# Adding the experts' weighted results into one row per token by indirect DMA

## The chip, the core and the metric

The kernel runs on one core of a Trainium2 chip. A core has a matrix engine (TensorE, PE in the profile; PEld is its weight load), VectorE (DVE), ScalarE (ACT), GpSimd (POOL) and SyncE (SP), which each run their own queue of instructions in order, and sixteen DMA engines that all queues share. DMAs issued by SyncE go out on a hardware queue (q1), those issued by GpSimd on a software queue (q0) whose descriptors GpSimd itself makes. The metric is the device time of one execution in microseconds (us), lower is better.

## The reference

The network has two layers on an image of 2 x 256 x 64 x 64: area attention and an LSTM, then convolutions with a state-space mixer, and at last a mixture of experts over the 8192 tokens. Only the last part is touched by the change:

```python
B, T, D, H, E = (16, 4096, 256, 512, 8)
xf = x.reshape(-1, Dd)
logits = xf @ gate_w + gate_b
probs = jax.nn.softmax(logits, axis=-1)
top2_vals, top2_idx = jax.lax.top_k(probs, 2)
cw = jnp.zeros((N, Ee)).at[jnp.arange(N)[:, None], top2_idx].add(top2_vals)
def step(acc, params):
    w1, bb1, w2, bb2, we = params
    h = jax.nn.gelu(xf @ w1 + bb1, approximate=False)
    y = h @ w2 + bb2
    return (acc + we[:, None] * y, None)
out, _ = jax.lax.scan(step, zeros_like(xf), (W1, b1, W2, b2, cw.T))
...
t = _to_tokens(x)
t = t + _L1_ffn_ref(_ln_t(t), ...)
x = _from_tokens(t, x)
```

The tokens are normalised, each goes to its two best of eight experts (256 to 512 to 256, GELU between), the two results are weighted by the softmax of the gate, summed and added to the token, and the tokens are turned back into channels by rows.

## The kernel before

`body` runs the attention, then the LSTM with the mixers, then `experts` (a second, conditional run of the last two exists for a guess that fails; it is skipped here). `experts` has three stages: `route`, `run_blocks`, `combine`. There T = 8192 tokens, P = 128 partitions, TILES = 64 tiles of 128 tokens, K = 4 tiles to a group, C = 256 channels.

**route.** `normalise` (L1949) turns the tokens group by group on TensorE, takes gate logits and statistics, and then `scale` (L2007) writes the normalised tokens: three tiles of a group on ScalarE, one on GpSimd, and one DMA of 0.52 MB by SyncE to the DRAM tensor `rows` (L2019). All sixteen `scale` groups stand after the second square root (L2084). `choose` picks the two best experts on VectorE. Then a table is built (L2221 to L2239) that says which token stands at which place: the assignments are sorted by expert into blocks of RB = 256 places, and one-hot products on TensorE, made by VectorE and ScalarE in sixteen rounds, fill `table`. Three blocks' weights are fetched before the table (L2210). `exponents` (L2109) comes behind it: ScalarE loads the exponential's table, makes the exponentials and loads GELU's. VectorE at last turns the table into the indices `xi` (rows to gather) and `ri` (rows to put).

**run_blocks(0, 68).** One block is 256 places of one expert; 2 x 8192 places need at most 71 blocks, of which 68 always run. The order is written out by hand. For block i TensorE does `turn` (transposes of the gathered rows `xg`), `up` (eight 128-row products into `ph`, GELU on ScalarE) and `down` (products into `py`); `up` of block i is interleaved with `down` of block i - 1. VectorE copies `xt` and adds the bias in `y`. GpSimd's queue has, for each block, the first put of 128 rows (L2323), the weights three blocks ahead (L2320, issued at L2125), the second put, and the two gathers of a later block (L2275). `results` has a row of its own for every (token, choice), and spare rows for empty places, so no two puts touch the same row: all are declared in one group "results" without dependences among them (L2328), and no put waits for another. Buffers: 3 for `xg`, 3 for `y`, 3 + 1 for the weights. During blocks 8 and 12 to 43 VectorE also computes the weights (`weigh`, L2116, sent through DRAM by two DMAs) and lays the tokens out by channels (`lay_out`, L2365).

**combine.** For each of sixteen groups of 512 tokens SyncE reads two tiles of `results` (both wait for all puts, L2380), ScalarE scales the first by its weight, VectorE multiplies and adds the second (L2387), TensorE transposes (L2391), VectorE adds the laid-out residual (L2397), and GpSimd issues the output's DMA (L2401).

Of the kernel before, what the change touches and what calls it, by code (L numbers as in the profile page):

```python
# [1861 lines left out]
def experts(tc, sh, ap, out, half, left):  # L1862
# [19 lines left out]
    with ExitStack() as ctx:  # L1882
        cp = ctx.enter_context(tc.tile_pool(name="e_const", bufs=1))
        dp = ctx.enter_context(tc.tile_pool(name="e_dram", bufs=1, space=bass.MemoryType.DRAM))
        rows = dp.tile([T, C], F32, name="rows")
        results = dp.tile([2 * T + NBLK * RB, C], F32, name="results")
        by_rows = dp.tile([T, 2], F32, name="by_rows")

        x = cp.tile([P, 2, WW, P], F32, name="x_turned")

        placed = sh.x.rearrange("p c b n -> p (c b n)").rearrange("p (c m w) -> p c m w", c=2, w=WW)

# [31 lines left out]
        weights = cp.tile([P, TILES, 2], F32, name="weights")  # L1924
        by_row = cp.tile([P, TILES // K, K, 2], F32, name="by_row")

        spare = iota("spare", [P, J, NBLK], [[P, J], [RB, NBLK]], base=2 * T + TILES, step=1)

# [20 lines left out]
        def normalise(p2, logits, halves):  # L1949


            with ExitStack() as own:
# [54 lines left out]
                def scale(g):  # L2007
                    xt = p2.tile([P, K, C], F32, name="xt")
                    for k in range(K):
                        t = g * K + k  # L2010
                        if k == K - 1:
                            nc.gpsimd.tensor_scalar(
                                xt[:, k], tok[:, t], inv[:, t : t + 1], less[:, t : t + 1], ALU.mult, ALU.add
                            )
                        else:
                            nc.scalar.activation(
                                xt[:, k], tok[:, t], AF.Identity, scale=inv[:, t : t + 1], bias=less[:, t : t + 1]
                            )
                    nc.sync.dma_start(rows.rearrange("(p w) d -> p w d", w=TILES)[:, group(g)], xt)  # L2019

# [29 lines left out]
                for g in range(TILES // K):  # L2050
# [24 lines left out]
                    if g == 13:  # L2075
                        ready = take_gates(*gates(2))
                        root_in(1)
                last = gates(3)
                root(1)
# [3 lines left out]
                turn_gates(*ready)  # L2083
                for g in range(TILES // K):  # L2084
                    scale(g)
# [23 lines left out]
        def exponents(pr):  # L2109

            nc.scalar.activation(one, going[:, 0, 0:1], AF.Exp)
            nc.scalar.activation(ex, pr, AF.Exp)
            nc.scalar.activation(best, best, AF.Exp)
            nc.scalar.activation(total[:, 0:1], sh.eps5, AF.Gelu)

        def weigh():  # L2116
            nc.vector.tensor_reduce(total, ex, AX.X, ALU.add)
            nc.vector.reciprocal(total, total)
            nc.vector.tensor_scalar(weights[:, :, 0], total, one, None, ALU.mult)
            nc.vector.tensor_tensor(weights[:, :, 1], best, total, ALU.mult)  # L2120
            nc.sync.dma_start(by_rows.rearrange("(p w) i -> p w i", w=TILES), weights)
            nc.sync.dma_start(by_row, by_rows.rearrange("(g p k) i -> p g k i", p=P, k=K))

# [11 lines left out]
        def route():  # L2135
            with ExitStack() as own:
# [12 lines left out]


                both = p1.tile(full, BF16, name="both")
                nc.vector.tensor_tensor(both, picks[0], picks[1], ALU.add)
# [56 lines left out]
                for i in range(3):  # L2209
                    fetch_weights(i)  # L2210


# [8 lines left out]
                for t0 in range(0, TILES, K):  # L2221
# [5 lines left out]
                    named = wide[t0 // K % 2][:, : 2 * size].rearrange("p (k i c n) -> p k i c n", k=K, i=2, c=2)  # L2227
                    nc.scalar.mul(named[:, :, :, 1], high.rearrange("p k n i -> p k i n"), me1)
                    for t in range(t0, t0 + K):
                        for i in range(2):  # L2230
# [9 lines left out]
                for _ in range(WARM_UP):  # L2240
                    nc.tensor.matmul(rest[:, :RB], every, place, start=True, stop=True)
                exponents(pr)
                tile_of, inner = (table[:, :, k * NB : k * NB + NBLK] for k in range(2))
                tokens = p1.tile([P, J, NBLK], F32, name="tokens")

                nc.vector.tensor_scalar(tokens, tile_of, float(TILES), float(T - TILES), ALU.is_ge, ALU.mult)
                nc.vector.tensor_tensor(tokens, tokens, tile_of, ALU.add)
                nc.vector.scalar_tensor_tensor(tokens, inner, float(TILES), tokens, ALU.mult, ALU.add)
# [3 lines left out]
                nc.vector.tensor_scalar(xi, ri, T - 1, None, ALU.bitwise_and)  # L2252

        puts = []
        landed = mybir.DependencyInfo(mybir.DependencyClass.Sync, mybir.DependencyReason.DATA)

        def run_blocks(lo, hi):
            with ExitStack() as own:
# [13 lines left out]
                def fetch(i):  # L2272
                    xg = fetched[i] = p3.tile([P, J, C], F32, name="xg")
                    for j in range(J):
                        gather(xg[:, j], rows, xi[:, j, i : i + 1])  # L2275

                def turn(i):
                    xg, wt = fetched.pop(i), weights_of.pop(i)
                    px = ps.tile([P, 2, RB], F32, name="px")
                    for c in range(2):  # L2280
# [4 lines left out]
                    if lo == 0 and i < 2:  # L2285
                        keep_busy(FILL + 2)
                    return xt, wt

                def up(xt, wt, alone):

# [11 lines left out]

                def down(i, act, wt, then):
                    py = ps.tile([P, J, C], F32, name="py")
# [11 lines left out]
                    nc.vector.tensor_tensor(y, py, b2, ALU.add)  # L2316
                    for j in range(J):

                        if j == 1 and then is not None:
                            fetch_weights(then, extra)  # L2320
                        elif j == 1 or then is None:
                            nc.gpsimd.memset(between, 0.0)
                        put = nc.gpsimd.indirect_dma_start(  # L2323
                            out=results, out_offset=bass.IndirectOffsetOnAxis(ap=ri[:, j, i : i + 1], axis=0),
                            in_=y[:, j], in_offset=None,
                        ).ins

                        tc.declare_no_dep(put, group="results", reason="different rows")  # L2328
                        tc.add_to_no_dep_group("results", put)
                        puts.append(put.name)  # L2330

# [6 lines left out]
                for i in range(lo, hi):  # L2338
# [16 lines left out]
                    for _ in below:  # L2355
                        pass
                    below = i, act, now[1]
                    if i == 8:
                        weigh()
                    if 12 <= i < 12 + 2 * T // TB:  # L2360
                        lay_out(*divmod(i - 12, 2))
                for _ in down(*below, None):
                    pass

        def lay_out(j, c):  # L2365

            rows_ = slice(j * TB // WW, (j + 1) * TB // WW)
            nc.vector.tensor_copy(placed[:, c, rows_], x[:, c, :, rows_].rearrange("p w m -> p m w"))

        def combine():  # L2370
            with ExitStack() as own:
# [3 lines left out]
                for g in range(T // TB):  # L2375
                    b, n0 = g * TB // N, g * TB % N
                    y = [p4.tile([P, K, C], F32, name=f"y{i}") for i in range(2)]
                    for i in range(2):
                        at = i * T + g * TB
                        got = nc.sync.dma_start(y[i], results[at : at + TB].rearrange("(p k) d -> p k d", k=K))  # L2380
                        for put in puts:
                            tc.add_manual_dep(got.ins, put, landed, reason="all results first")

                    po = ps.tile([P, 2, P, K], F32, name="po")
                    for k in range(K):
                        nc.scalar.activation(y[0][:, k], y[0][:, k], AF.Copy, scale=by_row[:, g, k, 0:1])
                        nc.vector.scalar_tensor_tensor(  # L2387
                            y[1][:, k], y[1][:, k], by_row[:, g, k, 1:2], y[0][:, k], ALU.mult, ALU.add
                        )
                        for c in range(2):  # L2390
                            nc.tensor.transpose(po[:, c, :, k], y[1][:, k, c * P : c * P + P], sh.ident)  # L2391
                    cut = slice(n0, n0 + TB)
                    res = p2.tile([P, 2, TB], F32, name="res")
                    before = placed[:, :, g * TB // WW : (g + 1) * TB // WW]
                    parts = [slice(0, 2)] if g < T // TB - 1 else [slice(0, 1), slice(1, 2)]
                    for eng, cs in zip((nc.gpsimd, nc.sync), parts):
                        nc.vector.tensor_tensor(  # L2397
                            res[:, cs], po[:, cs].rearrange("p c m k -> p c (m k)"),
                            before[:, cs].rearrange("p c m w -> p c (m w)"), ALU.add,
                        )  # L2400
                        eng.dma_start(out[b, :, cut].rearrange("(c p) n -> p c n", p=P)[:, cs], res[:, cs])  # L2401

# [149 lines left out]
```

## Time and profile before

| what | value |
|---|---|
| time, median of 3 runs | 2808.76 us (2808.6 to 2810.47) |
| the profiled execution's own time | 2817.78 us |
| its span, mean granted TensorE clock | 2815.9 us, 0.969 |
| DMA over the span | 399.14 MB, 142 GB/s |
| software queue q0 | 71488 packets, 293.00 MB, 44.1% of 16 engines |
| `experts`, from the first transposes to the end | about 2116 to 2816 us |
| first gather of `rows`, first put | 2206.62, 2232.84 us |
| `y<-results` issues | 32, of 512 KB, 2740.7 to 2786.0 us |

How to read it: an answer of the trace names an instruction by engine, line of the kernel, operation and tiles as `out<-in`; `xN` is how many. A time in brackets behind a row is how long the engine sat idle before it, and `<-` names what ended that wait. "Issue" is time in which an engine waited for nothing that the profile shows. The chain of waits follows the work that ended last back to its cause.

### The profile page before, as it was taken

Reading aid. Unit: us, or ns where it says so; the run is one execution under the profiler, and the core shown is the slowest. Engines: PE = TensorE matmul, PEld = TensorE weight load, DVE = VectorE, ACT = ScalarE, POOL = GpSimd, SP = SyncE. Lnnn points to the kernel's source line nnn. Section 1 sums busy time; section 2 is a strip of 40 time slices with the busy share of each in tenths; the row PEclk is TensorE's granted clock in tenths of the full one; section 3 lists DMA queues with packets and bytes.
Section 4 is the critical chain, followed back from the end, with each engine's and each line's share of the span. In section 5 each row is a group of like instructions: output and inputs, shape, how many; then the busy total and the mean of one; then the engine's idle time right before and its main releaser. Section 6 shows DMA issues by size and latency. Waiting matters only on the chain.

```text
span 2815.9 us, 45486 instructions
## 1 busy us (share of the span) xinstructions
PE 2582.6 (92%) x16873; PEld 1468.9 (52%) x16873; DVE 1921.1 (68%) x3693; ACT 1554.5 (55%) x2659; POOL 1276.2 (45%) x1214
## 2 busy tenths in 40 slices
PE   7899999999999999997899999868885899999984
PEld 2233333333333333331799999624444788888863
DVE  4788888888888888877666767698888322222116
ACT  2567677776777676664554555676637422222223
POOL 1354545444445545444312000287762366666651
PEclk9999999999999999999999999999997999999995
DMA  3566767676776767777450000045544266666658
GB/s 135 98 132 131 137 130 142 131 138 130 135 139 131 139 132 136 135 136 146 148 214 27 24 24 7 12 124 142 150 128 161 100 232 223 220 230 231 221 177 342
DMA packets 111226, 399.14 MB, mean 142 GB/s; under 512 B 20169, under 2 KB 24657, under 8 KB 101265
## 3 DMA queue, kind: packets, MB, share of 16 engines
q0 software_dynamic: 71488, 293.00, 44.1%
q1 hardware_dynamic: 38272, 98.87, 10.8%
q10 hardware_dynamic: 1232, 4.25, 0.4%
q8 instruction: 135, 2.21, 0.3%
q14 instruction: 99, 0.80, 0.1%
HBM read 178.81 MB, written 49.09 MB: 81 GB/s over the span
## 4 chain that ended last, share of the span: by engine, by line
PE 77%; DVE 10%; ACT 4%; issue 4%; DMA 3%; POOL 2%; SPq 0%; DVEq 0%; another core or an unknown queue 0%; POOLq 0%; ACTq 0%
PE ps L302 10%; PE ph L2296 9%; PE av_o L416 8%; PE po L170 8%; PE py L2308 8%; PE ps L403 7%; PE z L869 7%; PE z L829 6%; PE ps L398 3%; DVE hs L1744 2%; PE yp L1754 2%; DMA sx<-ex 2%; PE po L182 1%; DVE more L318 1%; PE po L416 1%
## 5 line engine op out<-in xcount | busy, mean ns | idle before, releaser
L372 DVE SCALAR_TENSOR_TENSOR acc<-vh,w_pe,acc 128x1008 f32<-128x1008 f32 (+7 forms) x384 | 482.2, 1259 | 8.3
L620 POOL DMA_DIRECT2D sx<-ex x320 | 279.6, 968 | 450.1 <-ACT ex L410 181.9
L410 ACT ACTIVATE ex<-ps 128x1024 f32<-128x1024 f32 x384 | 374.0, 1026 | 134.2 <-issue 54.3
L318 DVE CUSTOM_DVE_ANT_0 more<-ps,more 128x512 f32<-128x512 f32 x480 | 303.0, 687 | 132.1 <-PE ps L302 126.6
L2298 ACT ACTIVATE act<-ph,wt 128x256 f32<-128x256 f32 x272 | 129.2, 475 | 394.7 <-PE ph L2296 373.0
L2284 DVE COPY xt<-px 128x512 f32<-128x512 f32 x68 | 47.0, 692 | 395.7 <-PE px L2282 382.9
L2296 PE MATMUL ph<-xt,wt 128*128 128x256 f32 x1088 | 287.9, 387 | 5.5 <-ACT act L2298 4.0
L403 PE MATMUL ps<-q,k 32*128 32x512 f32 x2048 | 285.9, 600 | 0.0
L2308 PE MATMUL py<-wt,act 128*128 128x256 f32 x1088 | 278.7, 379 | 0.0
L615 POOL TENSOR_TENSOR sx<-sx,ex 128x1024 f32<-128x1024 f32 x64 | 153.1, 2391 | 221.2 <-PE ps L302 173.3
L314 ACT ACTIVATE more<-ps 128x1024 f32<-128x1024 f32 x240 | 233.5, 1029 | 16.7 <-ACT sx L410 5.9
L2296 PEld LDWEIGHTS ph<-xt,wt 128*128 128x128 f32 x1088 | 188.4, 189 | 66.1 <-DVE xt L2284 23.2
L416 PE MATMUL av_o<-ex,vt 128*32 128x512 f32 x1536 | 213.4, 608 | 6.2 <-ACT ex L410 6.2
L2308 PEld LDWEIGHTS py<-wt,act 128*128 128x128 f32 x1088 | 201.6, 190 | 24.7
L838 ACT ACTIVATE t<-z,bias 128x128 f32<-128x128 f32 x468 | 135.6, 365 | 124.2 <-PE z L869 122.8
L2323 POOL DMA_INDIRECT results<-y,ri x136 | 138.4, 1017 | 137.6 <-DVE y L2316 101.2
L302 PE MATMUL ps<-k,q 32*128 32x512 f32 x1088 | 183.4, 639 | 1.9 <-DVE nm L308 1.4
L869 PE MATMUL z<-xs,v 128*128 128x128 f32 x1512 | 180.9, 276 | 4.1 <-DVE xs L885 3.3
L829 PE MATMUL z<-xs,u 128*128 128x128 f32 x1536 | 183.5, 277 | 0.7 <-ACT xs L1003 0.7
L869 PEld LDWEIGHTS z<-xs,v 128*128 128x128 f32 x1512 | 174.1, 192 | 12.7 <-DVE xs L885 11.3
L829 PEld LDWEIGHTS z<-xs,u 128*128 128x128 f32 x1536 | 178.1, 193 | 0.9 <-ACT xs L1003 0.9
L1751 POOL TENSOR_TENSOR cs<-hs,cs 128x1024 f32<-128x1024 f32 x63 | 148.8, 2364 | 55.5 <-DVE hs L1744 37.1
(464 smaller groups left out, 4609.5 us busy)
## 6 DMA issues: line engine op xcount, KB each, us to landing
sx<-ex POOLq DMA_DIRECT2D x320, 512.0 KB
cs<-c_rows SPq DMA_DIRECT2D x128, 256.0 KB
y<-results SPq DMA_DIRECT2D x32, 512.0 KB
x<-xrows SPq DMA_DIRECT2D x8, 1024.0 KB
rows<-xt SPq DMA_DIRECT2D x16, 512.0 KB
out_x<-res POOLq DMA_DIRECT2D x15, 512.0 KB
xrows<-xn SPq DMA_DIRECT2D x24, 256.0 KB
u_rows<-xs SPq DMA_DIRECT2D x14, 384.0 KB
```

The source lines that it names most:

```text
L302: made.append(nc.tensor.matmul(tiles[h // 2][:, h % 2], qs[G, i // HM][head(h), i % HM * P : (i % HM + 1) * P], keys[head(h)], start=True, ...
L314: nc.scalar.activation(held["more"][j], tiles[j], AF.Relu)
L318: nc.vector.tensor_tensor_reduce(more, tiles[h // 2][:, h % 2], more, -1.0, 3.0e38, ALU.add, ALU.min, accum_out=nms[G][:, 0, h, i : i + 1],)
L372: mark(nc.vector.scalar_tensor_tensor(part, vh[:, c, 2 + r0 + dy : 2 + r1 + dy, w0 + dx : w1 + dx], w_pe[:, c, k : k + 1], part, ALU.mult, ...
L403: nc.tensor.matmul(tiles[h // 2][:, h % 2], k[head(h), m % HM * P : (m % HM + 1) * P], qs[G, n][head(h)], start=False, stop=True, tile_pos ...
L410: nc.scalar.activation(exs[i], tiles[i], AF.Exp, scale=HD**-0.5)
L416: nc.tensor.matmul(to[head(h)], lhs, exs[h // 2][:, h % 2], start=first, stop=last, tile_position=(0, HD * h))
L620: nc.gpsimd.dma_start(total[i], exs[i], accum_op=ALU.add)
L829: nc.tensor.matmul(z[c][:, g, :m], u[:, k, c, g], xin[j][:, k], start=g == GATES[0] and k == 0, stop=False, skip_group_check=True,)
L869: nc.tensor.matmul(z[c][:, g, :m], v[:, k, c, g], h[:, k], start=False, stop=k == 1, skip_group_check=True,)
L2296: nc.tensor.matmul(ph[:, hc], wt[:, at : at + P], xt[:, c], start=c == 0, stop=c == 1)
L2308: nc.tensor.matmul(py[:, j], act[:, hc, j * P : j * P + P], wt[:, at : at + C], start=hc == 0, stop=hc == NH - 1,)
```

## The change

Each token gets one row in `results`, which is filled with the token itself (the residual) before the blocks run (`keep_tokens`); the puts add into it by an accumulating indirect DMA. So `results` shrinks to 8192 rows and 256 spare ones. The weights of the two choices are computed on GpSimd in the table stage and stored in two more columns of `rows`, of which the second holds the difference of the weights; a gather brings them along, and VectorE scales `y` by the place's weight before the put. The puts of one block form a group, so that blocks are ordered among each other. Four `scale` groups and the exponentials move ahead. The combining stage reads one tile a group, transposes, and copies out on VectorE and ScalarE.

```diff
-        rows = dp.tile([T, C], F32, name="rows")
-        results = dp.tile([2 * T + NBLK * RB, C], F32, name="results")
-        by_rows = dp.tile([T, 2], F32, name="by_rows")
+        CW = C + 2
+        rows = dp.tile([T, CW], F32, name="rows")
+        results = dp.tile([T + RB, C], F32, name="results")
+        by_tile = rows.rearrange("(p w) d -> p w d", w=TILES)
...
-        spare = iota("spare", [P, J, NBLK], [[P, J], [RB, NBLK]], base=2 * T + TILES, step=1)
+        spare = iota("spare", [P, J, NBLK], [[P, J], [0, NBLK]], base=T + TILES, step=1)
+        second = cp.tile([P, J, NBLK], F32, name="second")
...
-                    nc.sync.dma_start(rows.rearrange("(p w) d -> p w d", w=TILES)[:, group(g)], xt)
+                    nc.sync.dma_start(by_tile[:, group(g), :C], xt)
...
                         root_in(1)
+                        scale(0)
+                for g in range(1, 4):
+                    scale(g)
                 last = gates(3)
...
-                for g in range(TILES // K):
+                for g in range(4, TILES // K):
                     scale(g)
...
-            nc.scalar.activation(total[:, 0:1], sh.eps5, AF.Gelu)
+            nc.scalar.activation(work[:, 0, 0:1], sh.eps5, AF.Gelu)
+            for n in (E // 2, E // 4, 1):
+                to = ex[:, :, :n] if n > 1 else total.unsqueeze(2)
+                nc.gpsimd.tensor_tensor(to, ex[:, :, :n], ex[:, :, n : 2 * n], ALU.add)
 
         def weigh():
-            nc.vector.tensor_reduce(total, ex, AX.X, ALU.add)
             nc.vector.reciprocal(total, total)
...
+            nc.gpsimd.tensor_scalar(weights[:, :, 0], total, one, None, ALU.mult)
+            nc.gpsimd.tensor_tensor(weights[:, :, 1], best, total, ALU.mult)
+            nc.gpsimd.tensor_tensor(weights[:, :, 1], weights[:, :, 1], weights[:, :, 0], ALU.subtract)
+            nc.gpsimd.dma_start(by_tile[:, :, C:], weights)
+
+        def keep_tokens():
+            for w in range(0, TILES, 8):
+                nc.sync.dma_start(results[:T].rearrange("(p w) d -> p w d", w=TILES)[:, w : w + 8], tok[:, w : w + 8])
+            nc.sync.dma_start(results[T:].rearrange("(j p) d -> p j d", p=P), tok[:, :J])
...
+                exponents(pr)
                 both = p1.tile(full, BF16, name="both")
...
                 for i in range(3):
                     fetch_weights(i)
+                keep_tokens()
...
+                    if t0 == 2 * K:
+                        weigh()
...
-                exponents(pr)
...
+                    share = p2.tile([P, J], F32, name="share", bufs=4)
+                    nc.vector.tensor_tensor(share, xg[:, :, C + 1], second[:, :, i], ALU.mult)
+                    nc.vector.tensor_tensor(share, share, xg[:, :, C], ALU.add)
...
                     for j in range(J):
+                        nc.vector.tensor_scalar(y[:, j], y[:, j], share[:, j : j + 1], None, ALU.mult)
...
-                            in_=y[:, j], in_offset=None,
+                            in_=y[:, j], in_offset=None, compute_op=ALU.add,
                         ).ins
-                        tc.declare_no_dep(put, group="results", reason="different rows")
-                        tc.add_to_no_dep_group("results", put)
-                        puts.append(put.name)
+                        tc.declare_no_dep(put, group=f"results{i}", reason="different rows")
+                        tc.add_to_no_dep_group(f"results{i}", put)
...
-                        nc.scalar.activation(y[0][:, k], y[0][:, k], AF.Copy, scale=by_row[:, g, k, 0:1])
-                        nc.vector.scalar_tensor_tensor(
-                            y[1][:, k], y[1][:, k], by_row[:, g, k, 1:2], y[0][:, k], ALU.mult, ALU.add
-                        )
...
+                    copies = nc.vector.tensor_copy, nc.scalar.copy
...
+                    for c in range(2):
+                        copies[c](res[:, c], po[:, c].rearrange("p m k -> p (m k)"))
```

More of the change, by code (lines that the diff above doesn't have):

```diff
@@ L1884, in experts @@
         dp = ctx.enter_context(tc.tile_pool(name="e_dram", bufs=1, space=bass.MemoryType.DRAM))
-        rows = dp.tile([T, C], F32, name="rows")
-        results = dp.tile([2 * T + NBLK * RB, C], F32, name="results")
-        by_rows = dp.tile([T, 2], F32, name="by_rows")
+        CW = C + 2
+        rows = dp.tile([T, CW], F32, name="rows")
+        results = dp.tile([T + RB, C], F32, name="results")
+        by_tile = rows.rearrange("(p w) d -> p w d", w=TILES)
         x = cp.tile([P, 2, WW, P], F32, name="x_turned")
-        placed = sh.x.rearrange("p c b n -> p (c b n)").rearrange("p (c m w) -> p c m w", c=2, w=WW)
         gate = cp.tile([P, 2, 32], F32, name="gate")
@@ L1924, in experts @@
         weights = cp.tile([P, TILES, 2], F32, name="weights")
-        by_row = cp.tile([P, TILES // K, K, 2], F32, name="by_row")
-        spare = iota("spare", [P, J, NBLK], [[P, J], [RB, NBLK]], base=2 * T + TILES, step=1)
+        spare = iota("spare", [P, J, NBLK], [[P, J], [0, NBLK]], base=T + TILES, step=1)
+        second = cp.tile([P, J, NBLK], F32, name="second")
         one = cp.tile([P, 1], F32, name="one")
@@ L2113, in exponents @@
             nc.scalar.activation(best, best, AF.Exp)
-            nc.scalar.activation(total[:, 0:1], sh.eps5, AF.Gelu)
+            nc.scalar.activation(work[:, 0, 0:1], sh.eps5, AF.Gelu)
+            for n in (E // 2, E // 4, 1):
+                to = ex[:, :, :n] if n > 1 else total.unsqueeze(2)
+                nc.gpsimd.tensor_tensor(to, ex[:, :, :n], ex[:, :, n : 2 * n], ALU.add)
         def weigh():
-            nc.vector.tensor_reduce(total, ex, AX.X, ALU.add)
             nc.vector.reciprocal(total, total)
[L2119 to L2122, printed above, removed]
+            nc.gpsimd.tensor_scalar(weights[:, :, 0], total, one, None, ALU.mult)
[6 more added lines that the diff above has]
+            nc.sync.dma_start(results[T:].rearrange("(j p) d -> p j d", p=P), tok[:, :J])
         def gather(dst, table, index):
@@ L2241, in route @@
                     nc.tensor.matmul(rest[:, :RB], every, place, start=True, stop=True)
-                exponents(pr)
                 tile_of, inner = (table[:, :, k * NB : k * NB + NBLK] for k in range(2))
                 tokens = p1.tile([P, J, NBLK], F32, name="tokens")
-                nc.vector.tensor_scalar(tokens, tile_of, float(TILES), float(T - TILES), ALU.is_ge, ALU.mult)
-                nc.vector.tensor_tensor(tokens, tokens, tile_of, ALU.add)
+                nc.vector.tensor_scalar(second, tile_of, float(TILES), None, ALU.is_ge)
+                nc.vector.scalar_tensor_tensor(tokens, second, -float(TILES), tile_of, ALU.mult, ALU.add)
                 nc.vector.scalar_tensor_tensor(tokens, inner, float(TILES), tokens, ALU.mult, ALU.add)
@@ L2252, in route @@
                 nc.vector.tensor_scalar(xi, ri, T - 1, None, ALU.bitwise_and)
-        puts = []
-        landed = mybir.DependencyInfo(mybir.DependencyClass.Sync, mybir.DependencyReason.DATA)
         def run_blocks(lo, hi):
@@ L2272, in fetch @@
                 def fetch(i):
-                    xg = fetched[i] = p3.tile([P, J, C], F32, name="xg")
+                    xg = fetched[i] = p3.tile([P, J, CW], F32, name="xg")
                     for j in range(J):
@@ L2286, in turn, with up @@
                         keep_busy(FILL + 2)
-                    return xt, wt
-                def up(xt, wt, alone):
+                    return xt, wt, share
+                def up(xt, wt, share, alone):
                     ph = ps.tile([P, NH, RB], F32, name="ph")
@@ L2301, in up, with down @@
                         yield act
-                def down(i, act, wt, then):
+                def down(i, act, wt, share, then):
                     py = ps.tile([P, J, C], F32, name="py")
@@ L2356, in run_blocks @@
                         pass
[L2357 to L2361, printed above, removed]
+                    below = i, act, *now[1:]
                 for _ in down(*below, None):
                     pass
-        def lay_out(j, c):
-            rows_ = slice(j * TB // WW, (j + 1) * TB // WW)
-            nc.vector.tensor_copy(placed[:, c, rows_], x[:, c, :, rows_].rearrange("p w m -> p m w"))
         def combine():
@@ L2376, in combine @@
                     b, n0 = g * TB // N, g * TB % N
[L2377 to L2382, printed above, removed]
+                    y = p4.tile([P, K, C], F32, name="y")
@@ L2384, in combine @@
+                    nc.sync.dma_start(y, results[g * TB : g * TB + TB].rearrange("(p k) d -> p k d", k=K))
                     po = ps.tile([P, 2, P, K], F32, name="po")
                     for k in range(K):
-                        nc.scalar.activation(y[0][:, k], y[0][:, k], AF.Copy, scale=by_row[:, g, k, 0:1])
-                        nc.vector.scalar_tensor_tensor(
-                            y[1][:, k], y[1][:, k], by_row[:, g, k, 1:2], y[0][:, k], ALU.mult, ALU.add
-                        )
@@ L2390, in combine @@
[L2390 to L2399, printed above, removed]
-                        )
-                        eng.dma_start(out[b, :, cut].rearrange("(c p) n -> p c n", p=P)[:, cs], res[:, cs])
+                        for c in range(2):
+                            nc.tensor.transpose(po[:, c, :, k], y[:, k, c * P : c * P + P], sh.ident)
@@ new lines, in combine @@
+                    res = p2.tile([P, 2, TB], F32, name="res")
+                    copies = nc.vector.tensor_copy, nc.scalar.copy
+                    last = g == T // TB - 1
+                    for c in range(2):
+                        copies[c](res[:, c], po[:, c].rearrange("p m k -> p (m k)"))
+                    for eng, cs in zip((nc.gpsimd, nc.sync), [slice(0, 1), slice(1, 2)] if last else [slice(0, 2)]):
+                        eng.dma_start(
+                            out[b, :, n0 : n0 + TB].rearrange("(c p) n -> p c n", p=P)[:, cs], res[:, cs]
+                        )
```

## The prediction

> **What bounds the kernel now.** I read the page's totals first, then the chain of waits, then the stretches by stage, then GpSimd's (POOL's) order of time in one block. The totals name TensorE:
>
> ```profile
> PE 2582.6 (92%) x16873; PEld 1468.9 (52%) x16873; DVE 1921.1 (68%) x3693; ACT 1554.5 (55%) x2659; POOL 1276.2 (45%) x1214
> ```
>
> That is an average over stages. Everything before about 2116 us is the same in both kernels, so only the experts' 700 us count. The chain in order of time (start, length, what) shows who holds the end there:
>
> ```profile
> 2709.09 1.05 PE ph L2296 x4
> 2716.64 1.05 PE ph L2296 x4
> 2725.19 0.97 POOL results L2323
> 2726.47 13.77 DMA results<-y,ri
> 2741.03 4.67 DMA y<-results
> 2746.56 1.98 PE po L2391 x8
> 2748.56 1.24 DVE res L2397
> 2751.17 2.58 issue
> 2754.53 2.90 issue
> ```
>
> Up to the last block TensorE leads, one `ph` piece every 7.55 us: a block takes 7.55 us. After that come the last puts, the first read of `results`, and sixteen groups of the combining stage, one per 3.69 us. Stretch by stretch (length, then busy time of the engines, granted clock, DMA share, GB/s):
>
> ```profile
> 2148.00:2172.00 24.00, 2.59 (x6) 0.70 (x7) 21.32 (x56) 23.96 (x50) 11.19 (x13) 0.56 0.78 317
> 2172.00:2206.00 34.00, 25.48 (x279) 23.40 (x279) 31.27 (x142) 33.51 (x149) 2.08 (x3) 0.91 0.35 130
> 2217.00:2734.00 517.00, 514.20 (x2458) 422.32 (x2459) 110.64 (x170) 128.90 (x272) 322.12 (x333) 1.00 0.61 216
> 2741.00:2804.00 63.00, 31.13 (x128) 22.17 (x128) 43.78 (x80) 27.34 (x64) 11.01 (x15) 0.50 0.97 389
> ```
>
> Normalising is ScalarE's, the slot table ScalarE's and VectorE's, the blocks TensorE's (514 of 517 us at full clock), and the combining stage has the DMA engines at 97%, with VectorE and TensorE taking turns right behind. In the blocks VectorE, ScalarE and the DMAs have room. POOL's order in one block decides what follows:
>
> ```profile
> 2247.95 0.99 POOL L2323 DMA_INDIRECT results<-y,ri  x1 [1.52 <-DVE y L2316]
> 2249.24 0.97 POOL L2125 DMA_INDIRECT wt<-in_Wall,wi  x1 [0.30 <-issue]
> 2250.52 0.99 POOL L2323 DMA_INDIRECT results<-y,ri  x1 [0.30 <-issue]
> 2251.82 0.97 POOL L2125 DMA_INDIRECT xg<-rows,xi  x1 [0.30 <-issue]
> 2253.09 0.95 POOL L2125 DMA_INDIRECT xg<-rows,xi  x1 [0.30 <-issue]
> 2255.50 0.99 POOL L2323 DMA_INDIRECT results<-y,ri  x1 [1.46 <-DVE y L2316]
> ```
>
> First put, the weights three blocks ahead, second put, two gathers; then POOL waits for VectorE. It is 1.5 us from being late, and it waits for no put.
>
> **The new wait in the blocks.** The change puts the puts of each block in a group of their own, and all add into the same `results`. In the new instruction order the first put of block b+1 therefore waits for the DMA semaphore of the second put of block b. Its price is when that second put lands. The page gives no landing times, but the trace's records of semaphore updates do: over the 64 blocks from 2232 to 2717 us the second put landed 5.15 us after its issue in the median, within 5.7 us in 42 blocks and around 8.2 us in most of the others, 6.09 us in the mean. It is this late because it stands in the queue behind 1.18 MB of weights issued 1.28 us earlier. With no traffic in front (the last two blocks) it took 2.38 us.
>
> So the new loop is: first put at T, second put at T + 2.57 (rows above), landed at T + 2.57 + 5.1 = T + 7.67. POOL then needs to wake: 0.19 us in the nearest case (a `rows` write landed at 2152.49, the POOL instruction that waited for it started at 2152.68), 0.29 us from VectorE's `y` (end 2247.66) to the put. I take 0.25. That is 7.92 us with the add free, against 7.55 today: the wait is already longer than the block.
>
> The late cases: in a late block the first put also lands at about 4.3 instead of 2.3 us, so one DMA engine came into the block 2 us behind. Draining the queue at each block removes those 2 us, and of 8.2 us some 6.2 remain. A third of the blocks with 1.0 us more is +0.35 on the mean. Ends: 0 (all quiet) and +0.99 (the mean of 6.09 stays).
>
> The add itself appears nowhere in this trace. Lower end 0. Upper end: every row is fetched in full before it is written, one after the other, 2.46 us (a gather on an idle queue landed 2.46 us after its issue, 2206.62 to 2209.10). I take it as the packets once more: a put is two packets of 4096 bytes for each DMA engine at 159 ns, so 0.32 us, plus the 0.1 to 0.2 us by which the idle gather landed later than an idle put; 0.5 us, because the queue hides latency but not occupancy. The Trainium skill speaks against a free add: "Collectives: The Full Stack", section "Why ReduceScatter is half of AllGather", says that an adding DMA reads two sources on one ring and so halves its rate. By that rule the add would cost 0.32 us, an estimate from the packet row, and no run here shows it.
>
> Period: 7.92 + 0.35 + 0.5 = 8.77, a lag of 1.22 us a block. Behind the waiting put stand the weights and gathers, and TensorE waits for those. The cover: the second gather of a block, issued at 2253.09, lands 3.2 us later when quiet, at 2256.3; its transposes come at 2260.6 (2245.8, 2253.0, then one block on). So 4.3 us of lag cost nothing. Sixty-three blocks have both the wait and a gather that depends on it: 63 x 1.22 - 4.3 = **+72.6 us**. Ends: 63 x 0.31 - 4.3 = +15 (period 7.86: free add, quiet, waking in 0.19 us), and 63 x 3.82 - 4.3 = +236 (period 11.37: all upper ends).
>
> The rest of a block is covered. VectorE gets two `share` products (0.17 us each by the 128x8 rows of the routing) and two scalings of 128x256 (between 0.26 us for 128x64, L2119, and 0.58 for 128x512, L1286; I take 0.37): 1.1 us a block, while VectorE is busy 111 of 517 us; one scaling delays the put by 0.37 us, which the later semaphore covers (in the last block it counts). Rows of 1032 instead of 1024 bytes in the gathers: under 1% more bytes, behind the second put. The 32 layout copies (19 us of VectorE) and the old weighing leave without gain, for the same reason.
>
> **Routing.** Four of sixteen groups of normalising move into ScalarE's idle time before 2148 (gaps of 1.86 and 4.61 us against 12 x 0.49 = 5.9): -5.9, with 0.4 for delaying the second square root. The exponentials now stand before the table: two table loads of 1.28, 0.61, 0.24 and two of 0.2 are 3.7 us. Behind the table these were covered by the gathers. VectorE's reciprocal (0.55) joins its queue in the table, where it is as full as ScalarE. POOL's three sums of the exponentials (2.39 us for 128x1024 in L1751, so about 1.1 for 256, 128 and 64 columns) stand before the first weights' gathers, which are not needed before 2212. Sum -5.9 + 0.4 + 3.7 + 0.55 = -1.3, say **-1**, between -2 (VectorE reaches the table at 2170.0 in any case) and +1.
>
> Two transfers are new here. The tokens' 8.65 MB go out behind `rows` on SyncE's queue, with 3.5 MB of weights beside them: 12.2 MB at 0.35 MB/us (a `rows` group of 0.52 MB every 1.48 us) are 34 us from about 2167, done by 2202, before the first gather (2206.6) and the first put (2232.8), which waits for them. Nothing stands behind them on SyncE before the combining stage. Uncovered they would stretch the first gathers by a few us. The weights go into 8192 runs of 8 bytes on POOL's queue, ahead of the gathers, which wait for their landing: 0.57 us for a 128-run output and 0.73 for 256 give 1.25 ns a run, 10 us. The old read of 2048 runs took 8.42 us to land under load; four times that is 34 at the upper end. Issued about 2178, landing between 2190 and 2222: 0 to +16 us. I take 0, since 1920 packets of it passed within 2 us once started. The skill's "DMA: Bandwidth & Descriptors", section "Specifications", says transfers under 512 bytes are read, modified and written; that would favour the upper end.
>
> **End.** Last block: one scaling 0.37, the add 0.5: **+1**. Combining: half the reads go (16 of 32 transfers of 0.52 MB), the output stays: 16.8 MB for 25.2. At 389 GB/s 43.1 us, where the loop took 64.3 (first read 2740.66 to last output 2804.96): **-21**. TensorE's 16 x 1.98 us plus 6 us of filling is 37.5, so -27 at best; at the 0.35 MB/us of the `rows` writes it is 47, -17.
>
> Sum: 72.6 - 1 + 1 - 21 = +51.6 on the profiled execution's 2817.78, which is 2869. That one stands 9.0 above the median of 2808.76, so on the median **2860 us**.
>
> **Rivals.**
> - *The add is nearly free and the queue quiet* (faster or the same). One mechanism: a drained queue lands each second put in 5.1 us, so the period is 7.86 to 7.92 and the lag +15 to +19, which the combining stage outweighs: 2803 at 7.86 (15 - 21 - 1 + 1 = -6), 2797 if combining also gains its 27, 2807 at 7.92. It decides below a period of 7.95, where 63 x 0.40 - 4.3 is 21. For: 42 of 64 quiet blocks. Against: any price of the add.
> - *The add is slow, row by row*: 2.46 us more than 8.27, period 10.73: 63 x 3.18 - 4.3 = +196, time 2984. For: each row is its own read and write. Against: gathers of scattered rows land nearly as fast as puts.
> - *The weights land late*: +16 us on the forecast, 2876; from the 8192 runs.
> - *The change doesn't do what it says*: the combining stage keeps 3.69 us a group, because copies and transposes still alternate; 2881. Against: the products that TensorE waits for (25.8 us) are gone.
>
> **How the numbers follow.** Forecast 0.55, free add 0.21, slow add 0.12, late weights 0.07, no gain in combining 0.05. Of the free add 0.13 ends below 2803 (combining between -21 and -27) and 0.08 within 0.2% (5.6 us, about what a measurement can tell from no change); the forecast's lowest corner adds 0.01 to the latter. So faster 0.13, same 0.09, slower 0.78. The forecast's own range, with the add from 0.2 to 1.2 us, is 2841 to 2904. To leave out no more than 2 in 10 I reach into the free add down to 2798 (period 7.86, combining at -26) and up to 2945 (period 10.1).
>
> **What would show it.** Right: POOL's first put waits for `results<-y,ri` in place of `y`; puts of successive blocks stand 8.3 to 9.5 us apart; TensorE idles about 1 us a block before the transposes; the combining loop takes about 43 us. Wrong: a block still takes 7.55 us, or the puts wait for `y`; the sum fails too if second puts land much later than 5.6 us or the first gather starts after 2210.

## The result and the profile after

The changed kernel takes **2977.55 us** (median of 5 runs, 2974.25 to 2990.39) against 2808.76 for the kernel before in the same comparison (2808.6 to 2817.64): a ratio of 1.059, 95% interval 1.057 to 1.061. The loss of 169 us is more than three times the 51 that were forecast, and the time lies above the stated upper end of 2945. The profiled execution took 2990.39 us, the slowest of the five; its span is 2988.6 against 2815.9. Later, beside other kernels, the same kernel had a ratio of 1.049 (1.047 to 1.051); the difference between the two occasions is taken up with that run.

Cut at three points that both traces have, the 172.7 us between the two spans are:

| stretch | before | after | difference | forecast |
|---|---|---|---|---|
| start to the load of the gate's bias (code unchanged) | 2115.7 | 2127.6 | +11.8 | 0 |
| to the first gather (routing) | 90.9 | 103.9 | +13.0 | -1 |
| to the first read of `results` (blocks and last puts) | 534.0 | 704.1 | +170.1 | +73.6 |
| to the end (combining) | 75.3 | 53.1 | -22.2 | -21 |

The first row lies within what executions differ by: the ten profiled ones of this document, whose code is the same up to there, reach this point between 2112.4 and 2127.6 us.

First the page's totals of the kernel after:

```profile
PE 2651.8 (89%) x16873; PEld 1498.5 (50%) x16873; DVE 1939.8 (65%) x3865; ACT 1537.9 (51%) x2611; POOL 1361.6 (46%) x1221
```

TensorE still has the largest share, and this says as little as it did before. The stretches do say something (span of the stretch, length, busy time of the engines in the order of the page, granted clock, DMA share, GB/s): the scaling, the blocks, the combining stage.

```profile
2160.00:2196.00 36.00, 6.07 (x36) 4.15 (x37) 23.51 (x67) 26.96 (x62) 12.12 (x17) 0.54 1.06 256
2256.00:2920.00 664.00, 557.39 (x2381) 433.86 (x2380) 156.77 (x392) 124.86 (x264) 399.88 (x329) 0.95 0.63 166
2935.00:2981.00 46.00, 26.13 (x128) 21.90 (x128) 11.07 (x16) 9.38 (x16) 11.57 (x16) 0.65 0.91 354
```

In the blocks TensorE is busy for 557 of 664 us, where it had 514 of 517; the DMA engines are at 63%, POOL at 60%. Nobody is full: the blocks are bound by waiting. GpSimd's order of time in one block shows for what:

```profile
2286.19 1.61 POOL L2336 DMA_INDIRECT results<-y,ri  x1 [2.52 <-DMA results<-y,ri]
2288.11 0.99 POOL L2135 DMA_INDIRECT wt<-in_Wall,wi  x1 [0.30 <-issue]
2289.40 1.59 POOL L2336 DMA_INDIRECT results<-y,ri  x1 [0.30 <-DVE y L2330]
2291.29 1.00 POOL L2135 DMA_INDIRECT xg<-rows,xi  x1 [0.30 <-issue]
2292.59 0.96 POOL L2135 DMA_INDIRECT xg<-rows,xi  x1 [0.30 <-issue]
2296.02 1.61 POOL L2336 DMA_INDIRECT results<-y,ri  x1 [2.47 <-DMA results<-y,ri]
```

The first put waits for the put before it, as forecast, and comes 9.83 us after the last one here. Two things are not as forecast: an adding put keeps GpSimd for 1.6 us where a plain one took 0.99, and the wait is 2.5 us long. The trace's semaphore records complete the loop, in medians: first to second put 3.20, issue of the second put to its landing 6.15, landing to the next block's first put 0.77. That is 10.12, the median period (mean 10.20). (A landing is the last semaphore update of a transfer, counted from the start of the instruction that issues it.)

Two groups of the page (busy time, mean ns of one, idle time before them and what ended most of it) show both ends of the delay:

```profile
L2336 POOL DMA_INDIRECT results<-y,ri x136 | 218.1, 1603 | 223.5 <-DMA results<-y,ri 151.2
L2289 DVE TENSOR_TENSOR share<-xg,second 128x2 f32<-128x2 f32 x68 | 12.0, 176 | 461.0 <-DMA xg<-rows,xi 461.0
```

Puts wait 151.2 us for puts; behind them in the same queue stand the gathers, so VectorE's `share`, the first user of gathered rows, waits 461 us for `xg`.

### The profile page after: what moved, and what is told of

It reads as the page before. It is cut to its first block, busy times and chain, and to the rows that moved or that the text cites. A ratio compares the mean times of both kernels' runs of the same rounds, so it can differ in the third digit from the quotient of the medians.

```text
span 2988.6 us, 45580 instructions
## 1 busy us (share of the span) xinstructions
PE 2651.8 (89%) x16873; PEld 1498.5 (50%) x16873; DVE 1939.8 (65%) x3865; ACT 1537.9 (51%) x2611; POOL 1361.6 (46%) x1221
## 5 line engine op out<-in xcount | busy, mean ns | idle before, releaser
L2336 POOL DMA_INDIRECT results<-y,ri x136 | 218.1, 1603 | 223.5 <-DMA results<-y,ri 151.2
L2289 DVE TENSOR_TENSOR share<-xg,second 128x2 f32<-128x2 f32 x68 | 12.0, 176 | 461.0 <-DMA xg<-rows,xi 461.0
L2308 PE MATMUL ph<-xt,wt 128*128 128x256 f32 x1088 | 302.3, 403 | 0.0
L2320 PE MATMUL py<-wt,act 128*128 128x256 f32 x1088 | 297.1, 399 | 0.0
L2308 PEld LDWEIGHTS ph<-xt,wt 128*128 128x128 f32 x1088 | 202.5, 200 | 59.5 <-DVE xt L2296 16.8
L2320 PEld LDWEIGHTS py<-wt,act 128*128 128x128 f32 x1088 | 213.8, 202 | 29.4
```

The costliest lines, as they stand in the source:

```text
L2308: nc.tensor.matmul(ph[:, hc], wt[:, at : at + P], xt[:, c], start=c == 0, stop=c == 1)
L2320: nc.tensor.matmul(py[:, j], act[:, hc, j * P : j * P + P], wt[:, at : at + C], start=hc == 0, stop=hc == NH - 1,)
L2336: put = nc.gpsimd.indirect_dma_start(out=results, out_offset=bass.IndirectOffsetOnAxis(ap=ri[:, j, i : i + 1], axis=0), in_=y[:, j], in_of ...
```

## The experiments

Periods are the distance of the first puts of successive blocks, mean of 61 and median; landings are medians.

**1 and 2. The add without the wait, the wait without the add.** Each puts one half of the change into the kernel before.

```diff
# e1_add_no_wait (results also filled with tokens beforehand)
-                            in_=y[:, j], in_offset=None,
+                            in_=y[:, j], in_offset=None, compute_op=ALU.add,
# e2_wait_no_add
-                        tc.declare_no_dep(put, group="results", reason="different rows")
-                        tc.add_to_no_dep_group("results", put)
+                        tc.declare_no_dep(put, group=f"results{i}", reason="different rows")
+                        tc.add_to_no_dep_group(f"results{i}", put)
```

> The kernel before with one thing changed: the puts add. Every (token, choice) keeps a row of its own, all puts stay in one group, so none waits for another. Adding needs rows that hold something, so all 34816 rows of results are filled with tokens at the start of the experts' stage (34.8 MB, some 100 us of transfers at 0.35 MB/us, which delays the writes of rows and the first gather); each result is therefore off by a token, and the total time is not the point, only the block period is. Theory (the wait for the landing costs, the add hardly): GpSimd's queue sets the pace, 2 x (1.60 + 0.30) + 3 x (0.98 + 0.30) = 7.64, so a period of 7.6 to 7.8 us against 7.55 before and 10.12 after. Rival (the add itself occupies queue and engines, the wait only shows it): a period of 8.5 us or more without any wait.

> The kernel before with one thing changed: the puts of one block are a group, so the first put of a block waits for the second of the block before; the puts are plain and go to rows of their own. Theory (the wait costs): first to second put 2.57, landing of the second 5.2 (median before) to 6.1 (mean before), then 0.77 until GpSimd starts: a period of 8.5 to 9.4 us, that is 63 x 0.95 - 4 = +56 to 63 x 1.85 - 4 = +112 us, 2865 to 2921 us in all. Rival (the add is what costs): a period of at most 7.8 us and at most 2825 us.

The add alone: period 7.74 mean, 7.67 median, and from the first gather to the first read of `results` 539.5 us against 534.0. (Its time, 2877.44 us in one run, holds the filling of all rows.) GpSimd in one of its blocks:

```profile
2407.20 0.98 POOL L2132 DMA_INDIRECT wt<-in_Wall,wi  x1 [0.30 <-ACT act L2306]
2408.49 1.59 POOL L2331 DMA_INDIRECT results<-y,ri  x1 [0.30 <-issue]
2410.39 1.39 POOL L2132 DMA_INDIRECT xg<-rows,xi  x1 [0.30 <-issue]
2412.08 0.95 POOL L2132 DMA_INDIRECT xg<-rows,xi  x1 [0.30 <-issue]
2413.33 1.61 POOL L2331 DMA_INDIRECT results<-y,ri  x1 [0.30 <-issue]
```

Each instruction starts 0.30 us behind the other: the queue is full, 2 x 1.90 + 3 x 1.28 = 7.64. The add costs almost nothing as long as nobody waits for its end.

The wait alone: 2888.84 us, ratio 1.026 (1.024 to 1.029); period 8.84 mean, 8.57 median; the block stretch 606.0, so +72.0.

```profile
2308.80 0.99 POOL L2323 DMA_INDIRECT results<-y,ri  x1 [2.61 <-DMA results<-y,ri]
2310.09 0.97 POOL L2125 DMA_INDIRECT wt<-in_Wall,wi  x1 [0.30 <-issue]
2311.37 0.99 POOL L2323 DMA_INDIRECT results<-y,ri  x1 [0.30 <-issue]
2312.66 0.97 POOL L2125 DMA_INDIRECT xg<-rows,xi  x1 [0.30 <-issue]
2313.93 0.94 POOL L2125 DMA_INDIRECT xg<-rows,xi  x1 [0.30 <-issue]
2317.48 0.99 POOL L2323 DMA_INDIRECT results<-y,ri  x1 [2.60 <-DMA results<-y,ri]
```

2.56 to the second put, 5.24 to its landing, 0.77 to the next put: 8.57. Both runs came out as expected, but the parts do not add up: 5.4 for the add and 72.0 for the wait are 77 of 170 us. The rest belongs to both together: inside the wait's loop the add's time is no longer covered. The next two runs show how much that is.

**3. The kernel after with plain puts, and unchanged.** The first shows whether the longer rows, the shares or the scalings have a part in it; the second stands beside it on the same chip.

```diff
# e6_after_no_add
-                            in_=y[:, j], in_offset=None, compute_op=ALU.add,
+                            in_=y[:, j], in_offset=None,
```

> The kernel after with plain puts in place of adding ones (so a token's row holds only the result put last). The wait stays, as do the 1032-byte rows, the shares and the scalings. If the period before + wait + add is all there is, the period is that of the kernel before with the wait alone: median 8.5 to 8.7, mean 8.7 to 9.0 us; first to second put 2.6, second landing 5.2. Rival (the longer rows or VectorE's scalings have a share in the block): a median above 8.9 us. Time about 2977 - 63 x 1.3 = 2895 us.

> The kernel after, unchanged, beside the others. The run with whole rows was 22 us faster than after, of which its routing (from the gate's loads to the first gather) explains 11.5 and its blocks, which the edit does not touch, 20 in the profiled executions (period 9.88 against 10.20). If that is the spread of one execution, this run shows a period of 9.9 to 10.2 and a ratio to before of 1.055 to 1.060; if the whole rows did change the blocks, a period of 10.15 or more here.

Without the add: period 8.82 mean, 8.57 median, the same 8.57 as with the wait alone, and 2877.98 us in one run. So the longer rows, the shares and the scalings cost no time in the blocks. The unchanged kernel on the same chip: 2961.22 us, ratio 1.049 (1.047 to 1.051), period 9.96 mean, 9.81 median. Between these two, on one chip, the add is worth 1.24 us a block: 0.64 between the puts (2.57 to 3.21) and 0.61 in the landing of the second (5.23 to 5.84).

The first part is GpSimd's: 1.60 us to issue the first put in place of 0.99. The second part is the DMA engines'. The second put's own issue takes 0.61 longer as well, but that is covered by the weights ahead of it: its first packet moves 5.10 us after the issue of the weights with the add and 5.06 without, when a first engine is through with the weights. Its last packet ends 6.75 and 6.12 us after that issue. For each engine an adding put has 8 packets of 1024 bytes at 102 ns, 0.82 us, where a plain one has 2 of 4096 at 159, 0.32.

Neither bound set for the repeat was met cleanly: the period falls into the spread that was named, the ratio lies below it. The second landing differs between the two occasions (6.15 and 5.84) because the weights ahead of it do: their last packet ends 6.34 us after their issue in the first and 6.06 in the repeat. Why the weights took longer is open.

**4. The weights behind both puts.**

```diff
-                        if j == 1 and then is not None:
-                            fetch_weights(then, extra)
-                        elif j == 1 or then is None:
+                        if j == 1 or then is None:
                             nc.gpsimd.memset(between, 0.0)
...
                         tc.add_to_no_dep_group(f"results{i}", put)
+                    if then is not None:
+                        fetch_weights(then, extra)
```

> The kernel after with one thing changed: the weights three blocks ahead are fetched behind the second put and not between the two (a small memset of one element stands between the puts). Theory (the second put lands late because it stands behind 1.18 MB of weights): put to put 2.2, landing 3.8 to 4.2 as with an idle queue, 0.77 to wake: 7.0 us, less than the 7.75 that GpSimd needs for its six instructions; a period of 7.7 to 7.9 us, and 63 x 2.4 = 150 us less than after, about 2825 us. Rival (the queue or the adding rows are slow whatever stands in front): landing stays above 5.5 us, the period above 8.8 us, the time above 2890 us.

2817.19 us, ratio to before 1.0014 (1.0002 to 1.0026); period 7.75 mean, 7.68 median.

```profile
2307.76 1.61 POOL L2334 DMA_INDIRECT results<-y,ri  x1 [0.30 <-issue]
2308.79 0.62 POOL L2333 MEMSET between<- 1x1 f32 x1
2309.68 1.60 POOL L2334 DMA_INDIRECT results<-y,ri  x1 [0.27 <-issue]
2311.59 1.00 POOL L2135 DMA_INDIRECT wt<-in_Wall,wi  x1 [0.30 <-issue]
2312.89 0.98 POOL L2135 DMA_INDIRECT xg<-rows,xi  x1 [0.30 <-issue]
2314.18 0.95 POOL L2135 DMA_INDIRECT xg<-rows,xi  x1 [0.30 <-issue]
2315.43 1.61 POOL L2334 DMA_INDIRECT results<-y,ri  x1 [0.30 <-issue]
```

The wait is still in the program, but it has ended before GpSimd comes to it: the second put is issued 1.92 behind the first and lands 3.84 later, and 1.92 + 3.84 + 0.77 = 6.53 is less than the 7.64 that GpSimd needs anyway. No put waits for `results` in the trace. Moving one instruction takes back the whole loss of the blocks but 12 us (545.8 against 534.0), and its mean period is that of the run with the add alone (7.75 and 7.74): GpSimd's own time.

**5. Whole rows.** Routing had lost 13 us (8.9 in the repeat: 99.8 against 90.9). In the kernel before each partition wrote four rows in one piece of 4096 bytes; with two columns left out between rows they became four pieces of 1024. This edit writes the two columns along:

```diff
-                    xt = p2.tile([P, K, C], F32, name="xt")
+                    xt = p2.tile([P, K, CW], F32, name="xt")
+                    nc.gpsimd.memset(xt[:, :, C:], 0.0)
...
-                    nc.sync.dma_start(by_tile[:, group(g), :C], xt)
+                    nc.sync.dma_start(by_tile[:, group(g)], xt)
```

> The kernel after with one thing changed: the tiles that are written to rows are 258 columns wide (the last two zero, overwritten by the weights later), so that each partition writes 4128 bytes in one piece and not four runs of 1024. Theory (the runs of 1024 bytes at a pitch of 1032 slow the writes): landing 2.6 to 3.5 us instead of 7.5, no waits of ScalarE for rows, its scaling done about 9 us earlier; the first gather, which waits for the weights' landing behind all that traffic, 3 to 10 us earlier; the time 2968 to 2975 us. Rival (the rows' starts off a multiple of 64 bytes are what slows): landing stays above 6 us, the time that of after, 2977.

ScalarE's order of time in the kernel before, where the 48 scalings run without a wait:

```profile
2148.27 23.71 ACT L2016 ACTIVATE xt<-x,less,inv 128x256 f32<-128x256 f32 x48
```

In the kernel after, a part of it:

```profile
2164.21 1.59 ACT L2015 ACTIVATE xt<-x,less,inv 128x256 f32<-128x256 f32 x3 [1.07 <-DMA rows<-xt]
2167.14 1.58 ACT L2015 ACTIVATE xt<-x,less,inv 128x256 f32<-128x256 f32 x3 [1.35 <-DMA rows<-xt]
2169.79 1.58 ACT L2015 ACTIVATE xt<-x,less,inv 128x256 f32<-128x256 f32 x3 [1.07 <-DMA rows<-xt]
```

In this experiment:

```profile
2153.11 4.53 ACT L2016 ACTIVATE xt<-x,less,inv 128x256 f32<-128x256 f32 x9
2158.32 17.78 ACT L2016 ACTIVATE xt<-x,less,inv 128x256 f32<-128x256 f32 x36
```

The writes land 2.80 us after their issue in place of 7.22, ScalarE's waits are gone, and from the gate's bias to the first gather it is 92.4 us, 7.5 to 11.5 less than in the two executions of the kernel after. So the four short runs per partition cost this time. The pieces start at multiples of 4128 bytes now, every second one 32 bytes off a multiple of 64, and the first four writes land alike (2.64, 2.61, 2.64, 2.64 us): a start 32 bytes off does not by itself slow these writes. Whether the short runs were slow by their length or by their number of unaligned ends, no run here separates. The time, 2955.77 us (ratio 1.050), comes from another comparison than either run of the kernel after, and these two differ by more than the gain; in the total it is not settled.

**6. Tokens early.**

```diff
+                keep_tokens()
                 with tc.tile_pool(name="e_n2", bufs=4) as p2:
...
-                keep_tokens()
```

> The kernel after with one thing changed: the tokens are written to results before the normalising, in the 30 us in which the DMA share is 0.00 to 0.03, and not behind rows. Theory (the weights land 33 us after their issue because the tokens' 8.65 MB stand in front of them): they land within 15 us, ScalarE still waits for rows as in after, and the first gather starts when the table is done, about 1 us behind xi: 3 to 4 us earlier than in after counted from the gate's loads (103.9 us there). Rival (8192 runs of 8 bytes are slow by themselves): landing stays above 25 us and the first gather where it was.

The weights land 15.8 us after their issue (31.3 in the unchanged kernel beside it), and the first gather starts 0.85 us after the table's last instruction, 97.9 us after the gate's bias in place of 99.8. That is half of the expected gain; the total, 2966.06 us, ratio 1.051 (1.049 to 1.053), is not better than the 1.049 beside it, so this edit alone is worth nothing that was measured. The landing behind the tokens is shown; its price on the path was 2 us.

**7. All repairs together**: experiments 4, 5 and 6, and the weights written by SyncE's queue.

```diff
-            nc.gpsimd.dma_start(by_tile[:, :, C:], weights)
+            nc.sync.dma_start(by_tile[:, :, C:], weights)
```

> Four repairs together on the kernel after: weights fetched behind the second put, whole rows of 1032 bytes, tokens written early, and the weights written by SyncE's queue in place of GpSimd's. Block period 7.7 to 7.8 (GpSimd's six instructions), from first gather to first read of results 546 us as with the weights last; from the gate's loads to the first gather 88 to 90 us (before 90.9, after 103.9); the end 53 us (before 75). Sum 88 + 546 + 53 = 687 against 700 for the kernel before: 12 us less, a ratio of 0.995 to 0.997 to before. If the ending or the routing does not add up, 1.000 to 1.003.

2813.60 us beside 2822.43 for the kernel before: ratio **0.9974** (0.9961 to 0.9986), a quarter of a percent less than the kernel before and 5% less than the kernel after beside it. Period 7.71; routing 89.6 us, blocks 547.8, end 57.5, together 694.9 where before has 700.2. The end fell 4.5 us short of what was expected (57.5 against 53); why is open. Its blocks, as one stretch:

```profile
2230.00:2740.00 510.00, 503.00 (x2380) 409.77 (x2379) 155.95 (x394) 124.55 (x263) 405.83 (x397) 1.00 0.81 216
```

TensorE is back at 503 of 510 us and at full clock.

## Why the prediction was wrong

**The wait: right in its place, short by two terms.** The prediction named the right instruction, the right semaphore and the reason why the second put lands late. Its sum for the period was 2.57 + 5.1 + 0.25 + 0.35 + 0.5 = 8.77; measured in the median: 3.20 + 6.15 + 0.77 = 10.12.

- *"Second put at T + 2.57".* This is the step that failed most. The sum kept the distance of two plain puts and looked for the add's price in the DMA engines alone, so GpSimd's longer issue of an adding put stood at nothing, without a reason. It takes 1.60 us in place of 0.99, and the distance became 3.20. 63 x 0.63 is 40 us.
- *"POOL then needs to wake", 0.25 us.* Measured 0.77, in every kernel that waits here. The rows taken for it were a computing instruction behind a DMA (0.19) and an indirect DMA behind VectorE (0.29); an indirect DMA that waits for a DMA was in neither. 63 x 0.52 is 33 us.
- *"The add itself", 0.5 us.* As a price in the DMA engines this was near: the landing came 0.61 later in the same-chip pair, though on an idle queue an adding put lands 1.39 later than a plain one (3.77 and 2.38). That the queue hides latency but not occupancy fits these numbers.
- *"Landed ... 5.1" and "late engine" +0.35.* The run with the wait alone has 5.24 and a mean 0.27 above the median: both near. With the add the mean is only 0.08 to 0.15 above the median. In the repeat the three terms of the landing sum to 5.99 (5.84 + 0.15) against 5.95 in the forecast, partly by luck: a later landing and fewer late blocks offset each other.

Without the add the whole stretch cost +72.0, close to the +72.6 forecast for wait and add together. That is luck: the short wake and the add that this run did not have cancel out.

In the kernel after the period's mean is 1.43 us above the forecast, and 63 x 1.43 = 90 of the 97 us by which the stretch missed. GpSimd's issue and the wake make 73 of these; the rest goes with the landing, which was 0.31 us later in this execution than in the repeat, behind slower weights.

**Routing, -1 forecast, +13 measured.** The step that failed is that the writes of `rows` were taken to cost what they did: "under 1% more bytes" was checked for the gathers, not for the writes, where a piece of 4096 bytes became four of 1024. Their landing went from 2.59 to 7.2 us and ScalarE ran out of `xt` buffers. The weights were put at 10 us, with 34 as the upper end; they landed 32.8 us after their issue behind the tokens and 15.8 without them, though GpSimd needed only 2.89 us to issue them. The forecast's cover, that the tokens are through by 2202, fell too: the last one landed at 2233.4. On the path the late weights were worth some 2 us, as experiment 6 shows. With whole rows, early tokens and the weights on SyncE's queue routing takes 89.6 us, 1.3 less than before: what the forecast had, once the writes cost what it assumed.

**Combining, -21 forecast, -22.2 measured.** Right in its reason: half the reads go, and the DMA engines are at 91% in the stretch above, where they were at 97%. The size is met with some luck. From the first read to the last output's issue it took 44.9 us (2935.51 to 2980.45) where 43.1 was forecast, so -19.4; the stretch above has 354 GB/s where the forecast took 389. Another 2.8 us went from what stands behind that issue (10.9 before, 8.1 after), which the forecast did not count. The two ends in the chain of waits:

```profile
2929.33 5.55 DMA results<-y,ri
...
2980.45 0.58 POOL out_x L2392
```

**The rivals.** "Free add and quiet queue" is excluded by the wait alone: its period is 8.57 in the median with no add at all, above the 7.95 at which it would have decided. "The add is slow, row by row" gave 2984 us, near the result, but by luck: it puts 2.46 us more on the second put's landing, and the same-chip pair shows 0.61. The 8192 runs did land late, and this was worth some 2 us and not 16. That the change would not do what it says fell with the combining stage.

The Trainium skill ("Collectives: The Full Stack", section "Why ReduceScatter is half of AllGather") spoke against a free add: two reads, half the rate. The direction agrees with the packets of the trace, 0.82 us for each engine where a plain put had 0.32. It says nothing of GpSimd's 0.61 us for each issue, which weighed as much.

## What to carry to other kernels

When a change makes one transfer wait for the end of another, write down the whole loop from issue to issue, and price in it every instruction that the issuing engine has to get through; a cost that was free under cover is paid wherever it stands in the loop uncovered, here ahead of the second put but not behind it. Then look at what stands in the queue ahead of the transfer that is waited for: moving 1.18 MB behind it shortened the blocks here by 146 us (692.2 to 545.8) to 158 us (704.1 to 545.8), and the wait itself could stay. When a row gets a wider pitch, check the writes as well as the reads, since what was one long piece falls apart.

## What the runs showed of the hardware that was not expected

- An adding indirect put of 128 rows of 1 KB takes GpSimd 1.60 us against 0.99 for a plain one, and on an idle queue lands 3.77 us after its issue against 2.38. Behind 1.18 MB of weights the difference in landing is 0.61.
- From the landing of a put to the start of the next put that waits for it: 0.77 us, against 0.19 for a GpSimd computing instruction behind a DMA and 0.29 for a put behind VectorE. In the 0.77 stand two semaphore instructions of GpSimd, 0.02 and 0.56 us after the landing; a put behind VectorE has one. Why the two are half a us apart is open.
- While GpSimd made the descriptors for the weights' 8192 runs (2.89 us), VectorE's one-hot comparisons, 0.28 us otherwise, took up to 2.48 us, in every kernel that wrote them from GpSimd; in the combined kernel, which writes them from SyncE, none did. The kernel after:

```profile
2197.67 2.89 POOL L2126 DMA_DIRECT2D rows<-weights  x1 [0.30 <-POOL weights L2125]
2197.74 0.28 DVE L2246 TENSOR_SCALAR picks<-place,lo 128x256 bf16<-128x256 bf16 x1
2197.93 0.28 DVE L2246 TENSOR_SCALAR left_upto<-place,lo 128x256 bf16<-128x256 bf16 x1
2198.13 2.48 DVE L2246 TENSOR_SCALAR picks<-place,lo 128x256 bf16<-128x256 bf16 x1
2198.32 2.35 DVE L2246 TENSOR_SCALAR left_upto<-place,lo 128x256 bf16<-128x256 bf16 x1
```
